# Storing u from ScalarE's queue, and moving late projections and splits, in a selective-scan and attention kernel

## The chip, the core and the metric

The kernel runs on one core of a Trainium2 chip. The metric is the device time of one execution in microseconds. Engines are named as in the profile: PE (TensorE), DVE (VectorE), ACT (ScalarE), POOL (GpSimd) and SP (SyncE, which here does nothing but issue DMAs).

## What is computed

An image batch x of shape (8, 64, 64, 96) goes through a state-space layer and then through an attention and feed-forward layer. The change lies in the first two of three passes, which compute this part of the reference:

```python
xz = jnp.einsum('bhwc,ec->bhwe', x, in_proj_w)          # x after a group norm
xin, z = jnp.split(xz, 2, axis=-1)
xc = jnp.transpose(xin, (0, 3, 1, 2))
xc = conv_general_dilated(xc, conv_w, ...) + conv_b      # depthwise, 3 x 3
xc = jax.nn.silu(xc)                                     # this is u
x_hw = xc.reshape(b, D_INNER, L)                         # row-major, o = 0
x_wh = jnp.transpose(xc, (0, 1, 3, 2)).reshape(b, D_INNER, L)   # column-major, o = 1
...                                                      # both, and both flipped: xs, K = 4
x_dbl = jnp.einsum('bkdl,kcd->bkcl', xs, x_proj_weight)  # dts, Bs, Cs
...
delta = jax.nn.softplus(dts + dt_projs_bias[None, :, :, None])
# the scan over L = 4096 steps, for 192 channels and 16 states
h = h * jnp.exp(d_t[..., None] * A) + (d_t * u_t)[..., None] * b_t[:, :, None, :]
y = jnp.einsum('bkdn,bkn->bkd', h, c_t)
```

The third pass (normalisation, gate, output projection, linear attention, quantised feed-forward layer) is the same in both kernels.

## The kernel before

**Three passes.** Pass 1 computes u, z and the projections x_dbl and puts them into DRAM. Pass 2 reads them back and does the scan. Pass 3 does the rest.

**Chunks.** Batches are taken in four pairs. The 192 channels of two batches make three chunks of 128 partitions (`chunk_rows`): chunks 0 and 1 hold the first 128 channels of one batch each ("one-batch chunks"), chunk 2 the last 64 channels of both ("two-batch chunk").

**Pass 1.** `projection` loads x, normalises it, multiplies by the input weights and copies the result into padded images (`xpad`, ScalarE) and z. `convolution` does nine multiply-adds on VectorE per chunk, in the order 0, 2, 1 within a pair, into one of four u buffers; then silu in two halves on ScalarE, then copies of u with rows and columns exchanged, in windows of 16 columns (`ut`, ScalarE; at the last chunk VectorE does them). `storage` stores the `ut` windows and then u itself in four column pieces, all through SyncE's queue. `x_projection` multiplies u by the projection weights on TensorE, ScalarE copies the product (`xd`), and SyncE stores it (`xd_d`). `split` loads rows of `xd_d`, makes three bf16 parts of them on ScalarE and GpSimd (`bq`, `bs`) and stores them (`b_d`, `dt_d`) for pass 2. A convolution takes a u buffer of four chunks earlier, and so waits until that chunk is stored and its x_proj is done. xpad, in turn, is free for the next pair when the convolution that read it is over.

**Pass 2.** It goes through 4 pairs x 3 chunks x 4 directions x 4 pieces of 1024 steps = 192 pieces, each with 16 states. For each piece: loads of the bf16 B rows (`xb`), of u, of `xdt`, and of C rows broadcast over the partitions (`c`); delta and the decay `da` (ScalarE); delta times u times B (`x`, `xg`, or on VectorE `wide`); the scan `h` (VectorE); h times C (`c<-c,h`, GpSimd); and the sum over the states on TensorE (`acc`). A two-batch chunk has the same work per piece, but loads each thing for two halves of the partitions and so issues twice the DMAs.

**Late work.** Some of pass 1's work is done within pass 2. The x_proj of batch 7 is there (`late_x_projection`, 16 units of 512 steps: three loads of u, four matmuls, a copy, a store), and so are the splits of batches 4 to 7 (`late_split`, 24 units). They belong to a kind "split" of which one unit is open at a time.

**What sets the order.** Each engine's instructions have a fixed order, written by a planner at build time (`weave`). The program parts are Python generators that name an engine, a cost and a delay before each step. Of all steps that could begin, `weave` takes the one that begins first by these costs; of those that begin at the same time, the one with the lower rank. In pass 1 the rank is the place of the unit's kind in the dictionary `room` (which also says how many units of a kind may be open), then its place in the list. In pass 2 the rank is a number: step n of piece `at` has about `at * N + n`, with N = 16, so a pair spans 768, a chunk 256. All of it concerns order alone; on the chip semaphores decide when an instruction begins. All engine instructions are issued by one helper, so the profile gives them one line, L93, and they are told apart by the names of their tiles.

Of the kernel before, what the change touches and what calls it, by code (L numbers as in the profile page):

```python
# [43 lines left out]
NB, HH, WW, C = 8, 64, 64, 96  # L44
L = HH * WW
DI, N, R, K = 192, 16, 6, 4
# [4 lines left out]
T = 1024  # L51
# [18 lines left out]
def chunk_rows(pair, c):  # L70

    b0 = 2 * pair
    if c < 2:
        return [(slice(0, P), b0 + c, slice(0, P))]
    return [(slice(64 * j, 64 * j + 64), b0 + j, slice(P, DI)) for j in range(2)]
# [225 lines left out]
def pass1(ctx, tc, g, a_neg, constants, ident, mhalf, engines, w_xp, u_d, z_d, xd_d, b_d, dt_d):  # L301
    nc = tc.nc
    pe, dve, act, pool = engines
    sp = InOrder(tc, nc.sync)
# [66 lines left out]
    sts, gms, us, turned, done = {}, {}, {}, {}, {}  # L371
# [115 lines left out]
    def convolution(pair, c):  # L487

        ty = c // 2
        src = xpad[c + pair % 2 if c == 2 else c]  # L490
        if pair == 0:
            yield ("parameters",)
        halves = 2 if pair == 0 and c == 0 else 1
        if halves == 1:
            for b in [2 * pair, 2 * pair + 1] if c == 2 else [2 * pair + c]:
                yield "proj", b
        before = {0: (pair - 1, 1), 2: (pair, 0), 1: (pair, 2)}[c]
        at = 3 * pair + ORDER.index(c) - UB
        if at >= 0:
            old, c_old = at // 3, ORDER[at % 3]  # L500
            for b in {0: (2 * old,), 1: (2 * old + 1,), 2: (2 * old, 2 * old + 1)}[c_old]:
                yield "xproj", b
            yield "stored", old, c_old
        if before[0] >= 0:
            yield "conv", *before
        u = None
        for part in range(halves):
            if halves > 1:
                for q in range(NG):
                    if q * RPG < (part + 1) * HH // halves + 1:  # L510
                        yield "projected", 0, q
            rows = slice(part * HH // halves, (part + 1) * HH // halves)
            for tap in range(9):
                end = yield "dve", (2.55 if tap == 0 else 4.55) / halves, 0.0
                if u is None:
                    u = us_p.tile([P, L], F32, name="u", tag=f"u{(at + UB) % UB}")
                    us[pair, c] = u
                    uv = u.rearrange("p (h w) -> p h w", w=WW)
                win = src[:, tap // 3 + rows.start : tap // 3 + rows.stop, tap % 3 : tap % 3 + WW]
                if tap == 0:  # L520
                    dve.tensor_scalar(uv[:, rows], win, conv_w[:, ty, tap : tap + 1], None, ALU.mult)
                else:
                    dve.scalar_tensor_tensor(uv[:, rows], win, conv_w[:, ty, tap : tap + 1], uv[:, rows], ALU.mult, ALU.add)
        done["conv", pair, c] = end
        for h in range(2):
            cols = slice(h * (L // 2), (h + 1) * (L // 2))
            end = yield "act", 2.0
            act.activation(u[:, cols], u[:, cols], AF.Silu, bias=conv_b[:, ty, :])
        done["u", pair, c] = end
        for i, (w, by_vector) in enumerate(windows(pair, c)):  # L530
            wide = w.stop - w.start
            tag = f"xn{i - 2}"
            step = ("dve", wide * 0.07, 0.3) if by_vector else ("act", 2.0, 0.3)
            if i < 2 or not by_vector:
                end = yield (*step, uts)
                tag = f"ut{uts.taken}"
            else:
                end = yield step
            turned[pair, c, i] = ut_p.tile([P, wide * HH], F32, name="ut", tag=tag), uts.taken
            (dve.tensor_copy if by_vector else act.copy)(turned[pair, c, i][0].rearrange("p (w h) -> p h w", h=HH), uv[:, :, w])  # L540
            done["turned", pair, c, i] = end

    def windows(pair, c):

        if (pair, c) == (NB // 2 - 1, ORDER[-1]):
            ends = (0, 16, 32, 40, 48, 56, 64)
        else:
            ends = (0, 16, 32, 48, 64)
        return [(slice(*at), len(ends) > 5) for at in zip(ends, ends[1:])]

    def storage(pair, c):

        parts, slow = chunk_rows(pair, c), 1 + c // 2 * 0.7
        for i, (w, by_vector) in enumerate(windows(pair, c)):
            yield "turned", pair, c, i
            end = yield "sp", 1.9 * (w.stop - w.start) / 16 * slow
            ut, of_ut = turned[pair, c, i]
            for part, b, ch in parts:
                sp.dma_start(u_d[b][1][ch, w.start * HH : w.stop * HH], ut[part, :])
            if i < 2 or not by_vector:  # L560
                uts.release(of_ut, end + 2.5)
        for i in range(4):
            cols = slice(i * T, (i + 1) * T)
            end = yield "sp", 1.9 * slow
            for part, b, ch in parts:
                sp.dma_start(u_d[b][0][ch, cols], us[pair, c][part, cols])
        done["stored", pair, c] = end + 2.5

    def x_projection(b, o, q):
        pair, j = b // 2, b % 2  # L570
# [32 lines left out]
    units = []  # L603
    for pair in range(NB // 2):
        batches = (2 * pair, 2 * pair + 1)
        for b in batches:
            units += [("stats", statistics(b, q)) for q in range(NG)]
            units.append(("norm", group_norm(b)))
            units += [("proj", projection(b, q)) for q in range(NG)]
        for c in ORDER:  # L610
            units.append(("conv", convolution(pair, c)))
            units.append(("store", storage(pair, c)))
        for b in batches:
            for o in range(2 if b < LATE_X else 0):
                units += [("xproj", x_projection(b, o, q)) for q in range(NG)]
                if b < LATE:
                    units += [("split", after(("xd", b, o), split((act, pool, sp), (two, two), 4.4, 4.0, xd_d[b][o], *w))) for w in splits(b, o, b_d, dt_d)]
    units += [("early", early_loads()), ("later", later_loads())]
    parts_of = [partial(us_p.tile, tag=f"u{UB - 1 - i}") for i in range(2)]
    units.append(("constants", make_constants(sp, dve, *parts_of, done)))  # L620
    room = {"early": 1, "proj": 4, "norm": 1, "stats": 5, "xproj": 4, "split": 2, "conv": 3, "store": 3, "later": 1, "constants": 1}
    weave([(kind, (list(room).index(kind), i), unit) for i, (kind, unit) in enumerate(units)], room, done)


# [1 line left out]
def pass2(ctx, tc, g, ident, engines, fixed, w_xp, u_d, xd_d, b_d, dt_d, y_d):  # L626
# [3 lines left out]
    pe, dve, act, pool = engines  # L630
    sp = InOrder(tc, nc.sync)
    room = {"da": 4, "h": 3, "x": 4, "xg": 1, "c": 6, "wide": 3, "acc": 1}
# [126 lines left out]
    def late_x_projection(b, o, q):  # L759

        yield "scans", 0
        pair, j = b // 2, b % 2
        cols = slice(q * GRP, (q + 1) * GRP)
        yield "sp", 1.8, 12.0
        ux = wide_late.tile([P, 2, GRP], F32, name="ux", tag="wide")
        sp.dma_start(ux[:, 0, :], u_d[b][o][0:P, cols])
        for i in range(2):
            sp.dma_start(ux[64 * i : 64 * i + 64, 1, :], u_d[2 * pair + i][o][P:DI, cols])
        yield "pe", 1.5, 0.2, slots["wide"]
        px, slot = take("wide", [P, T])  # L770
        for i, ty in enumerate((0, 1 + j)):
            pe.matmul(px[:, 0:GRP], w_xp[:, ty, o, :], ux[:, i, :], start=i == 0, stop=i == 1)
        end = yield "act", 0.58, 0.2
        xd = late_p.tile([P, GRP], F32, name="xd", tag="narrow")[0 : 2 * NXD]
        act.copy(xd, px[0 : 2 * NXD, 0:GRP])
        slots["wide"].release(slot, end)
        end = yield "sp", 0.7, 25.0
        sp.dma_start(xd_d[b][o][:, cols], xd)
        one_more(("xd", b, o), NG, end)

    def late_split(b, o, which):

        yield "scans", 0
        if b >= LATE_X:
            yield "xd", b, o
        yield from split((act, pool, sp), (late_p, wide_late), 1.25, 12.0, xd_d[b][o], *which)
        one_more(("split", b), 6, 0.0)
# [198 lines left out]
    units = []  # L986
# [23 lines left out]
                add("sum", -6, sum_over_n(at, n // 2), n)  # L1010
        add("acc", -2, take_acc(at), N)
    late_x = [(b, o, q) for b in range(LATE_X, NB) for o in range(2) for q in range(NG)]
    late = [("split", 3 * N * (i + 1), late_x_projection(*which)) for i, which in enumerate(late_x)]
    last = [(b, o, w) for b in range(LATE, NB) for o in range(2) for w in splits(b, o, b_d, dt_d)]
    late += [("split", 5 * N * (i + 1), late_split(*which)) for i, which in enumerate(last)]
    units += sorted(late, key=lambda unit: unit[1])
    weave(units, {"soft": 1, "prep": 1, "c": 1, "da": 2, "x": 1, "xg": 1, "dbu": 3, "scan": 3, "carry": 1, "term": 1, "sum": 1, "acc": 1, "split": 1}, done, keep_busy)

# [328 lines left out]
```

## Time and profile before

| | us |
|---|---|
| median of 3 runs (range) | 9731.19 (9728.52 to 9740.45) |
| the profiled execution, its own time | 9741.73 |
| its span in the profile | 9740.0 |
| DVE busy in the span | 9287.6 (95%) |
| ACT busy | 9098.2 (93%) |
| POOL busy | 8982.4 (92%) |
| PE busy | 7931.2 (81%) |
| first scan of pass 2 begins | 669.5 |
| last scan ends | 9056.3 |

Busy times are of the engines proper; issuing a DMA is not counted. Slices of the page divide the span into 40 equal parts, and a digit is the busy share in tenths. In lists of waits a row names the engine and the tile that an instruction writes, then what released it, and gives the total, the number of times and the longest. In timelines, the first two numbers are the start and the length in microseconds, and the bracket gives the idle time before the instruction and what ended it. `u_d<-u` are row-major stores of u, `u_d<-ut` those of the exchanged copies, `xd_d<-xd` those of x_proj.

### The profile page before, as it was taken

Reading aid. Unit: us, or ns where it says so; the run is one execution under the profiler, and the core shown is the slowest. Engines: PE = TensorE matmul, PEld = TensorE weight load, DVE = VectorE, ACT = ScalarE, POOL = GpSimd, SP = SyncE. Lnnn points to the kernel's source line nnn. Section 1 sums busy time; section 2 is a strip of 40 time slices with the busy share of each in tenths; the row PEclk is TensorE's granted clock in tenths of the full one; section 3 lists DMA queues with packets and bytes.
Section 4 is the critical chain, followed back from the end, with each engine's and each line's share of the span. In section 5 each row is a group of like instructions: output and inputs, shape, how many; then the busy total and the mean of one; then the engine's idle time right before and its main releaser. Section 6 shows DMA issues by size and latency. Waiting matters only on the chain.

```text
span 9740.0 us, 163473 instructions
## 1 busy us (share of the span) xinstructions
PE 7931.2 (81%) x57252; PEld 6142.7 (63%) x57252; DVE 9287.6 (95%) x6986; ACT 9098.2 (93%) x21482; POOL 8982.4 (92%) x2903
## 2 busy tenths in 40 slices
PE   7768888888888888888888888888888888888787
PEld 4336666666666666666666666666666666666676
DVE  8879999999999999999999999999999999999688
ACT  6669999999999999999999999999999999999787
POOL 1449999999999999999999999999999999999677
PEclk9879999999999999999999999999999999999898
DMA  6677776799987777799976767899867767999763
GB/s 179 211 233 226 235 236 225 239 224 209 217 224 224 230 231 226 237 211 214 214 232 221 237 217 226 228 211 210 224 222 233 227 220 230 219 208 214 195 183 111
DMA packets 945110, 2120.78 MB, mean 218 GB/s; under 512 B 278476, under 2 KB 426733, under 8 KB 944291
## 3 DMA queue, kind: packets, MB, share of 16 engines
q1 hardware_dynamic: 939394, 2108.50, 78.2%
q8 instruction: 458, 7.50, 0.3%
q14 instruction: 362, 2.96, 0.1%
q10 hardware_dynamic: 4464, 0.88, 0.1%
q0 software_dynamic: 432, 0.94, 0.0%
HBM read 1934.36 MB, written 175.66 MB: 217 GB/s over the span
## 4 chain that ended last, share of the span: by engine, by line
ACT 32%; DVE 24%; issue 17%; POOL 10%; PE 10%; DMA 6%; SPq 1%; DVEq 0%; POOLq 0%; ACTq 0%
DVE h L93 19%; ACT x L93 13%; ACT da L93 11%; POOL c L93 8%; PE wide L93 3%; DVE wide L93 3%; PE acc L93 3%; DMA c<-xd_d 2%; DMA xb<-b_d 1%; PE pa L93 1%; DMA xd_d<-xd 1%; ACT y L93 1%; ACT L93 1%; ACT delta L93 1%; ACT duT L93 1%
## 5 line engine op out<-in xcount | busy, mean ns | idle before, releaser
L93 POOL TENSOR_TENSOR c<-c,h 128x2048 f32<-128x2048 f32 x1536 | 6962.5, 4562 | 69.7 <-DVE h L93 48.7
L93 DVE TENSOR_TENSOR_SCAN h<-da,carry,wide 128x1024 f32<-128x1024 f32 x2304 | 5243.0, 2328 | 82.5 <-PE wide L93 39.6
L93 ACT ACTIVATE x<-duT,bT 128x128 f32<-128x128 f32 (+1 forms) x14336 | 4231.4, 368 | 2.1
L93 ACT ACTIVATE da<-delta,a_neg 128x1024 f32<-128x1024 f32 x3072 | 3508.2, 1146 | 171.2 <-DVE h L93 161.9
L93 PE MATMUL acc<-ident,c 128*128 128x128 f32 x24576 | 3132.4, 276 | 351.6 <-POOL c L93 342.6
L93 PEld LDWEIGHTS acc<-ident,c 128*128 128x128 f32 x24576 | 2762.0, 142 | 801.8 <-POOL c L93 687.5
L93 PE MATMUL wide<-ident,x 128*128 128x128 f32 x11264 | 1506.2, 277 | 418.9 <-DVE h L93 322.0
L93 DVE TENSOR_TENSOR_SCAN h<-da,wide 128x1024 f32<-128x1024 f32 x768 | 1704.9, 2268 | 43.6 <-PE wide L93 28.5
L93 PEld LDWEIGHTS wide<-ident,x 128*128 128x128 f32 x11264 | 1251.8, 142 | 690.6 <-DVE h L93 176.3
L93 DVE TENSOR_TENSOR wide<-du,wide 128x1024 f32<-128x1024 f32 x1216 | 1456.7, 1209 | 50.1 <-PE wide L93 47.5
L93 PE MATMUL acc<-sel,zero 96*128 96x512 bf16 x4100 | 1130.4, 380 | 0.0
L93 PE MATMUL wide<-xb,sel 96*128 96x512 bf16 x2432 | 722.8, 381 | 303.4 <-DVE h L93 263.8
L93 POOL TENSOR_TENSOR xg<-duT,bT 128x512 f32<-128x512 f32 (+1 forms) x640 | 895.9, 1417 | 20.5 <-ACT duT L93 20.5
L93 PE MATMUL wide<-ident,xg 128*128 128x128 f32 x3584 | 483.3, 279 | 153.8 <-DVE h L93 139.1
L93 PEld LDWEIGHTS <-zero 96*128 96x128 bf16 x4100 | 398.4, 98 | 317.2 <-issue 3.3
L93 PEld LDWEIGHTS wide<-ident,xg 128*128 128x128 f32 x3584 | 401.9, 143 | 244.4 <-issue 192.0
L93 PEld LDWEIGHTS <-sel 96*128 96x128 bf16 x2432 | 221.0, 98 | 498.0 <-issue 297.8
L93 POOL TENSOR_TENSOR du<-delta,u 128x1024 f32<-128x1024 f32 x192 | 458.3, 2387 | 29.2 <-DMA u<-u_d 27.0
L93 DVE SCALAR_TENSOR_TENSOR u<-xpad,conv_w,u 128x4096 f32<-128x4096 f32 (+1 forms) x104 | 446.1, 4290 | 2.4
L93 ACT ACT_TABLE_LOAD x197 | 252.8, 1283 | 38.2 <-DMA u_d<-u 22.8
L93 PE MATMUL wide<-ident,du 128*128 128x128 f32 x1536 | 204.7, 276 | 81.6 <-DVE h L93 65.1
L93 PE MATMUL px<-u,w_xp 128*128 128x512 f32 x448 | 216.1, 625 | 41.8 <-ACT u L93 21.0
(148 smaller groups left out, 6045.4 us busy)
## 6 DMA issues: line engine op xcount, KB each, us to landing
c<-xd_d SPq DMA_DIRECT2D x1024, 1024.0 KB
c<-xd_d SPq DMA_DIRECT2D x1024, 512.0 KB
u<-u_d SPq DMA_DIRECT2D x127, 512.0 KB
xdt<-dt_d SPq DMA_DIRECT2D x1146, 36.0 KB
xb<-b_d SPq DMA_DIRECT2D x382, 96.0 KB
u<-u_d SPq DMA_DIRECT2D x128, 256.0 KB
zs<-z_d SPq DMA_DIRECT2D x128, 256.0 KB
y_d<-y SPq DMA_DIRECT2D x96, 256.0 KB
```

Source lines behind the costliest of these rows:

```text
L93: ins = getattr(self.engine, op)(*args, **kwargs).ins
```

## The change

There are three edits in pass 1 and one in pass 2.

1. `storage` no longer stores row-major u. `convolution` does it, right behind the silu and ahead of the exchanged copies, from ScalarE's queue, with one DMA for a one-batch chunk (2 MB) and two for a two-batch chunk (1 MB each). The planner is told 0.7 us per issue and a delay of 10 us until the buffer counts as stored.
2. The storage units of the first three pairs get a place in `room` ahead of x_proj, split and conv. Those of the last pair become a kind of their own, "close", behind conv.
3. The late x_proj of batch 7 is ranked at `N * (1.9 * i + 1)`, so from 16 to 472: within the one-batch chunks of pair 0. Before, ranks went from 48 to 768, over the whole pair.
4. The late splits of batches 4 and 5 are ranked from 768 to 1208, those of 6 and 7 from 1536 to 1976: within the one-batch chunks of pairs 1 and 2. Before, the 24 ranks went from 80 to 1920 in steps of 80.

```diff
@@ convolution
         done["u", pair, c] = end
+        parts = chunk_rows(pair, c)
+        end = yield "act", 0.7 * len(parts), 10.0
+        for part, b, ch in parts:
+            act.dma_start(u_d[b][0][ch], u[part])
+        done["stored", pair, c] = end
@@ storage
-        for i in range(4):
-            cols = slice(i * T, (i + 1) * T)
-            end = yield "sp", 1.9 * slow
-            for part, b, ch in parts:
-                sp.dma_start(u_d[b][0][ch, cols], us[pair, c][part, cols])
-        done["stored", pair, c] = end + 2.5
@@ pass1
-            units.append(("store", storage(pair, c)))
+            units.append(("store" if pair < NB // 2 - 1 else "close", storage(pair, c)))
...
-    room = {"early": 1, "proj": 4, "norm": 1, "stats": 5, "xproj": 4, "split": 2, "conv": 3, "store": 3, "later": 1, "constants": 1}
+    room = {"early": 1, "proj": 4, "norm": 1, "stats": 5, "store": 3, "xproj": 4, "split": 2, "conv": 3, "close": 3, "later": 1, "constants": 1}
@@ pass2
-    late = [("split", 3 * N * (i + 1), late_x_projection(*which)) for i, which in enumerate(late_x)]
+    late = [("split", N * (1.9 * i + 1), late_x_projection(*which)) for i, which in enumerate(late_x)]
     last = [(b, o, w) for b in range(LATE, NB) for o in range(2) for w in splits(b, o, b_d, dt_d)]
-    late += [("split", 5 * N * (i + 1), late_split(*which)) for i, which in enumerate(last)]
+    late += [("split", N * (48 * (i // 12 + 1) + 2.5 * (i % 12)), late_split(*which)) for i, which in enumerate(last)]
```

## The prediction

> **What bounds the kernel now.** I read the page's slices first, then the busy times of stretches cut at the pass borders, then who waits for whom inside pass 1, then the chunks of pass 2. The slices show three regimes:
>
> ```profile
> DVE  8879999999999999999999999999999999999688
> ACT  6669999999999999999999999999999999999787
> POOL 1449999999999999999999999999999999999677
> ```
>
> The stretches give them sizes (columns: length, busy us of PE, PEld, DVE, ACT, POOL, clock, DMA share, GB/s):
>
> ```profile
> 493.00:626.00 133.00, 83.99 (x187) 35.71 (x188) 120.00 (x28) 87.77 (x101) 34.85 (x16) 0.80 0.66 211
> 626.00:670.00 44.00, 13.24 (x52) 7.93 (x51) 7.05 (x12) 13.86 (x14) 4.29 (x4) 0.65 0.80 257
> 670.00:9056.00 8386.00, 6908.20 (x51688) 5447.00 (x51688) 8229.67 (x4286) 8129.90 (x19578) 8292.70 (x2414) 0.99 0.82 224
> ```
>
> Pass 2 is 8386 of 9740 us, and there VectorE, ScalarE and GpSimd are all near 98%: only a stage with idle time of all three can give anything. Pass 1 (to about 670) has no full engine: the chain runs through VectorE's convolutions (39 us a chunk) and whatever holds the next one up. From 626 to 670 nobody works and the DMA engines are at their densest: pass 1 ends in a drain of stores. The change touches nothing after 9056.
>
> What VectorE waits for in pass 1 (total us, times, longest):
>
> ```profile
> DVE u L93 <- ACT xpad L93: 20.8, 3, 9.6
> DVE u L93 <- DMA u_d<-u: 18.3, 2, 13.0
> ```
>
> What ScalarE waits for there:
>
> ```profile
> ACT xd L93 <- DMA xd_d<-xd: 54.6, 41, 6.4
> ...
> ACT ut L93 <- DMA u_d<-ut: 32.4, 18, 5.7
> ACT L93 <- DMA u_d<-u: 22.8, 1, 22.8
> ```
>
> So late stores stop VectorE directly, and stop ScalarE, whose xpad copies VectorE waits for. The last row is the end of the pass, in ScalarE's timeline:
>
> ```profile
> 635.49 3.89 ACT L93 ACTIVATE u<-u,conv_b 128x2048 f32<-128x2048 f32 x2
> ...
> 664.64 1.28 ACT L93 ACT_TABLE_LOAD   x1 [22.83 <-DMA u_d<-u]
> ```
>
> The last silu ends at 639.4, and the first decay of pass 2 waits until the last row-major u store has landed at 664.6.
>
> **Part 1, the u store on ScalarE's queue.** Removed from SyncE: 32 issues of 512 KB and 32 of 256 KB. Added on ScalarE: 8 issues of 2 MB and 8 of 1 MB, right behind the silu. The bytes are the same.
>
> Where the stores stand on the path. (a) Today they come far behind their silu: chunk 2 of pair 1 had its silu at 281 and was stored between 372 and 447. The convolution that takes its buffer (pair 2, chunk 1) stands 13.0 us for it, and starts at 451.5. Stored behind the silu that wait is gone; next late is the x_proj of batch 3, which reads the same buffer until about 435, and VectorE is busy with statistics to 438.5. So I take all 13 us. The other store waits of a convolution (5.3 us at 498.6, 3.6 at 333.0) are worth nothing: the convolution after each starts late anyway, because xpad is late (6.5 and 9.6 us).
> (b) Between the end of each pair's last convolution and the middle chunk of the next pair lie 177.3-232.9, 329.4-384.5 and 493.4-548.7, each 55 us, with ScalarE busy 42 to 48 of 56. ScalarE is the chain there; its waits for landings in them add to 3.8, 8.5 and 5.3, together 17 us (x_proj stores, split loads, transposed stores, all on SyncE's queue). With 64 issues fewer on that queue, and the transposed stores ranked ahead of x_proj, I take two thirds: 12 us.
> (c) The end. From 635.9 SyncE issues 6.5 MB of stores, landed at 664.6: 28.7 us, about 237 GB/s. Of these, 2 MB are row-major u of chunk 2, whose silu was over at 600; they now leave before the last convolution ends, under which the DMA share is 0.66. 4.5 MB remain, 20 us at the same rate, so the landing comes near 658: 7 us. The last silu itself stands 10 us behind its convolution, behind x_proj copies that wait for their stores 1.5 us each; those stores stay, so I give that 2 us. Together 9 us.
>
> What it costs ScalarE. The only issues of this kind in the trace are SyncE's:
>
> ```profile
> L93 SPq DMA_DIRECT2D u_d<-u x64: 341/706/2702, 123.5 to 658.3; - x64
> ```
>
> An issue takes 0.3 to 2.7 us. A 2 MB issue isn't in the trace; 1 MB loads of c issue in 0.4 us when nothing is in the way, so size is not what sets it, congestion is. And there is a new wait: in the trace's DMA records SyncE's and ScalarE's issues take eight completion semaphores in turn, and each stands until the last transfer on its semaphore has landed. Stores of 512 KB landed in 3.5 to 8.8 us, median 5.2, by those semaphores. So an issue on ScalarE may cost from 0.3 us (the eighth transfer before it has landed) to 11.5 us (8.8 + 2.7). Behind it are queued the transposed copies, xpad, xn and z of the next batch, and the x_proj copies, and TensorE and VectorE wait for those. I take 2.7 us, an issue at its dearest but rarely a landing, because ScalarE comes to its store some 4 us after the convolution's end. One such store lies in each of the stretches of (b): 3 x 2.7 = 8 us; those outside are covered by ScalarE's 30 to 40% idle time under convolutions. In turn SyncE's eighth issue behind a 2 MB store waits for it; SyncE waited 197 us for ScalarE in pass 1, which covers that.
>
> A rule speaks against all this. The Trainium skill (DMA: Bandwidth & Descriptors, section "Issuing engines are not separate DMA queues") says that transfers started by different engines run on the same 16 DMA engines and interleave, so another issuer saves only issue time. By it (a) to (c) hold only as far as the *order* of stores changes, and SyncE's saved issue time (64 x 0.7 = 45 us) is on no path: taken strictly 0 us. The rows decide for the order: the 13.0 us wait is for a store 91 us or more behind its silu, at a DMA share of 0.69. Where the share is 0.80, at the end, I follow the rule and count bytes only.
>
> Pass 1: 13 + 12 + 9 - 8 = 26 us less. Ends: 13 + 17 + 21 with no cost, some 50 less; and below nothing, see the rivals.
>
> **Part 2, late work in one-batch chunks.** Pass 2 by chunk, cut at the first scan of each:
>
> ```profile
> 1358.80:2042.90 684.10, 569.61 (x4307) 449.25 (x4305) 679.41 (x354) 660.47 (x1474) 682.66 (x184) 1.00 0.75 234
> 2042.90:2789.80 746.90, 604.25 (x4359) 467.00 (x4359) 699.49 (x370) 720.37 (x1969) 717.34 (x246) 0.97 0.98 214
> ...
> 5574.50:6255.30 680.80, 562.61 (x4299) 446.99 (x4297) 678.72 (x353) 655.59 (x1463) 675.51 (x177) 1.00 0.73 226
> 6255.30:6975.30 720.00, 589.62 (x4317) 456.26 (x4316) 699.49 (x370) 710.82 (x1948) 710.77 (x240) 0.99 0.98 214
> ```
>
> The first and third are one-batch chunks (pairs 0 and 2), the second and fourth two-batch ones. Pair 0's two-batch chunk takes 746.9 us, pair 2's 720.0, with VectorE equally busy (699.5): 26.9 us of plain idle time. Only the first carries late work (5 late x_proj, 3 splits). Two-batch chunks run at a DMA share of 0.98: the late 5 x 0.5 MB of u, 0.9 MB of xd and 1.8 MB of splits are 5.2 MB, 24 to 25 us at 214 GB/s (1 MB a little over 10^6 bytes). SyncE's waits there agree:
>
> ```profile
> SPq L93 <- DMA xd_d<-xd: 24.4, 4, 9.4
> ...
> SPq L93 <- ACT xd L93: 11.1, 3, 4.3
> SPq L93 <- DMA b_d<-bs: 7.6, 1, 7.6
> ```
>
> Behind these SyncE holds the xb and u of the next piece, for which all three engines stand 5 to 6 us at 2254, 2290 and 2569. The change puts none of this there: 26 us saved.
>
> What it costs elsewhere. Pair 0's one-batch chunks lose 6 splits and take 16 x_proj instead of 11, each 4 matmuls and one copy of 0.6 us, with ScalarE idle 24 us and the DMA share 0.75: nothing by the row at 1358.8, which with 5 x_proj and 3 splits is only 3.3 us over the empty chunk at 5574.5. So without splits they win 3.3 us each, 6.6. A split is 2 x 1.17 us on GpSimd, which has 5 us to spare in an empty chunk. Pair 1's one-batch chunks with 6 splits each take 691.0 and 689.0 against 682.8 and 680.7 in pair 3: 8.3 us for 6, 1.4 a split. Twelve splits now fall on pair 1's (7 and 5 by rank, as before about 12) and twelve on pair 2's (before 2): about 10 more at 1.4, 13 to 14 us. Sum: 26 + 6.6 - 13.5 = 19 us less. Ends: 8 (x_proj every 30 ranks instead of 48 disturbs its chunks) and 27 (splits fall into ScalarE's and GpSimd's gaps).
>
> **The sum.** The profiled run is 9741.7 us with a span of 9740.0; it is 10.5 over the median of 9731.2. 26 + 19 = 45: a span near 9695, and 9731 - 45 = 9686 as a median. A measurement of this kernel tells about 0.2%, 19 us, from no change.
>
> **Rivals.**
> - *Order buys nothing in pass 1* (the rule strictly, or ScalarE pays as much as it wins): only part 2, 9712, within 0.2%. For it: the same bytes, a DMA share near 0.7. Against: the 13.0 us wait at 451. Chance 0.17.
> - *The queue was the pass's real limit*: ScalarE's 105 us of waits for x_proj stores, transposed stores and split loads mostly go, 55 us in pass 1 with part 2 at 24: 9652. Chance 0.2.
> - *Late work is moved, not removed*: one-batch chunks pay the 26 us back; pass 1 alone, 9705. Against: the 3.3 us of the chunk at 1358.8. Chance 0.12.
> - *Slower*: ScalarE stands at its store for a semaphore whose transfer SyncE issued late. Price up to 11.5 us; half of the 16 issues on the path are 92 us, against 34 + 19 won: 9770. It decides from 53 / 8 = 6.6 us a store. For it: SyncE's issues take up to 3.9 us in bursts. Against: a median landing of 5.2 us. Chance 0.08.
> - My forecast has 0.43, with 9665 to 9705 as its own range.
>
> Faster by over 0.2%: 0.43 + 0.2 + 0.12 = 0.75; within 0.17; slower 0.08. The range 9645 to 9722 takes in the first three rivals at their values and leaves out the slower one and the far end of the second.
>
> **What would show it.** The convolution now at 451.5 starts behind x_proj, not behind a u store; ScalarE's waits for landings fall from 105 us; the gap now 22.8 before the first decay is about 15; the first scan, now at 669.5, comes near 644; pair 0's two-batch chunk takes about 720 us, pair 2's one-batch chunks 687 to 692. I am wrong if ScalarE shows long gaps before its u stores, or if the three 55 us stretches grow.

## The result and the profile after

The changed kernel takes 9709.1 us (median of 12 runs, 9699.6 to 9720.1) against 9732.4 for the kernel before (12 runs beside it). The ratio is 0.9975, 95% interval 0.9966 to 0.9984: 23 us less, between 16 and 33. The forecast was 45 less.

Both profiled executions lie some 10 us above their medians (9720.1 and 9741.7), so they can be set beside each other. The slices of the page after hardly differ from before:

```profile
DVE  8879999999999999999999999999999999999687
ACT  5669999999999999999999999999999999999787
POOL 1459999999999999999999999999999999999777
```

Cut at the last convolution, the first scan and the last scan (columns as before):

```profile
493.00:633.00 140.00, 91.00 (x210) 39.46 (x208) 120.23 (x26) 85.04 (x110) 64.51 (x18) 0.82 0.65 194
633.00:673.50 40.50, 7.29 (x40) 5.51 (x40) 8.63 (x12) 17.35 (x19) 11.41 (x14) 0.58 0.82 245
673.50:9038.60 8365.10, 6901.12 (x51737) 5444.10 (x51738) 8231.73 (x4288) 8127.22 (x19575) 8289.72 (x2414) 0.99 0.82 224
```

Pass 2 is 21.7 us shorter (8386.8 to 8365.1), with the same busy times. In these two executions pass 1 is not shorter at all: its last convolution ends at 632.9 instead of 625.7 and the first scan begins at 673.5 instead of 669.5. In the first stretch GpSimd is busy 64.5 us instead of 34.9. One execution is a weak witness for a few microseconds: the work behind the last scan, which is the same in both kernels, differs by 3.9 us here (683.7 and 679.8), and a second execution of the same pass 1, in run a2 below, began its first scan at 664.0.

The four chunks of pass 2 that answer to those shown before (pair 0, then pair 2, each the second one-batch chunk and the two-batch chunk):

```profile
1361.50:2046.20 684.70, 573.93 (x4331) 455.25 (x4330) 679.74 (x354) 658.53 (x1470) 676.40 (x179) 1.00 0.74 233
2046.20:2764.90 718.70, 586.35 (x4337) 451.46 (x4338) 699.18 (x370) 712.65 (x1951) 714.00 (x243) 1.00 1.00 215
5547.80:6237.90 690.10, 570.28 (x4322) 455.07 (x4320) 679.86 (x353) 661.51 (x1480) 687.89 (x188) 0.99 0.72 228
6237.90:6959.20 721.30, 596.50 (x4324) 466.59 (x4322) 699.26 (x370) 714.01 (x1954) 712.16 (x241) 0.97 0.98 214
```

The second row is the gain: 746.9 to 718.7. The third is the price, 680.8 to 690.1, in a chunk that now does splits on GpSimd (675.5 to 687.9 busy). Both repeat: the eleven other runs with the new late ranks have 716.7 to 721.5 and 689.5 to 690.4 there, and a2, with the old ones, 741.2 and 681.1. SyncE's waits in the second row's chunk no longer hold a row for `xd`, `xd_d` or `bs`. In pass 1, VectorE's waits from 60 to 670:

```profile
DVE u L93 <- ACT xpad L93: 38.2, 3, 18.8
DVE ut L93 <- DMA u_d<-ut: 27.0, 2, 13.7
```

The row `DVE u <- DMA u_d<-u` (18.3 us before) is gone, and that for xpad has grown by 17.4 (20.8 to 38.2): almost the same time is now waited for something else. ScalarE's waits up to 670:

```profile
ACT xd L93 <- DMA xd_d<-xd: 57.9, 31, 10.4
ACT bs L93 <- DMA bq<-xd_d: 32.4, 9, 8.4
...
ACT ut L93 <- DMA u_d<-ut: 15.9, 11, 3.6
...
ACT delta L93 <- PE wide L93: 14.8, 1, 14.8
```

Fewer stores on SyncE's queue did not shorten the waits for x_proj's stores (54.6 to 57.9). Those for exchanged stores halved (32.4 to 15.9), and those for split loads nearly doubled (17.8 to 32.4). The new issues are cheap; among the rows that touch `u_d`, with durations in ns as least/median/most:

```profile
L93 ACTq DMA_DIRECT2D u_d<-u x16: 321/416/1310, 93.6 to 645.4; - x16
```

**Where the lead goes.** In the kernel before, the convolution at 498.6 ended at 542.2; now it runs from 486.8 to 526.9. So at that point VectorE is 15.3 us ahead: step (a) arrived there in full. Its timeline after that point, before:

```profile
548.72 2.36 DVE L93 TENSOR_SCALAR u<-xpad,conv_w 128x4096 f32<-128x4096 f32 x1 [6.54 <-ACT xpad L93]
551.11 36.13 DVE L93 SCALAR_TENSOR_TENSOR u<-xpad,conv_w,u 128x4096 f32<-128x4096 f32 x8
...
```

and after:

```profile
545.75 2.35 DVE L93 TENSOR_SCALAR u<-xpad,conv_w 128x4096 f32<-128x4096 f32 x1 [18.85 <-ACT xpad L93]
548.14 40.77 DVE L93 SCALAR_TENSOR_TENSOR u<-xpad,conv_w,u 128x4096 f32<-128x4096 f32 x8
...
592.11 40.79 DVE L93 SCALAR_TENSOR_TENSOR u<-xpad,conv_w,u 128x4096 f32<-128x4096 f32 x8
```

x8 are the eight multiply-adds of one convolution. The lead falls from 15.3 to 3.0 us in one wait for xpad (18.85 us instead of 6.54), and to 7.2 us behind in two convolutions whose multiply-adds take 5.10 us in the mean (40.77 / 8) instead of 4.52. Taken one by one, twelve of the sixteen last 5.26 us and four 4.49; before, all sixteen lasted 4.49. Beside these two convolutions GpSimd now does splits, the last of which begins at 643.5; before, the last began at 546.3.

Why xpad comes hardly earlier than before stands in the chain of waits of the kernel after (start, length, what):

```profile
370.39 11.28 DMA xt<-in_x
...
520.47 9.66 DMA xt<-in_x
```

These are loads of x, issued by SyncE; 2 MB stores of u had left ScalarE's queue at 367.0 and 516.9. TensorE's projection waits for them, and xpad for the projection. Over pass 1, by the completion semaphores of the trace, the 7 loads `xt<-in_x` issued from 1 us before to 5 us after a u store land in 9.8 us on average, the other 37 in 3.9; the stores of z in 10.4 (12 of them) and 4.1. Before, with u stores of 256 and 512 KB, both groups of loads took 3.7 to 3.8. So the load at 520.5 explains some 6 of the 12.3 us by which the lead shrank in the wait for xpad; the rest of them is not traced.

The chain as a whole, in shares of the stretch from 330 to the first scan, before:

```profile
by line: DMA xd_d<-xd 25.1%; PE pa L93 17.6%; PE px L93 11.5%; DMA u_d<-ut 8.0%; ACT ut L93 4.8%; ACT u L93 4.6%; SPq L93 4.1%; issue 4.1%; PE pt L93 3.6%; DMA bq<-xd_d 2.3%; DMA c<-xd_d 2.2%; DMA u<-u_d 2.2%; ACT xd L93 2.1%; ACT z L93 1.6
```

and after:

```profile
by line: SPq L93 15.5%; PE pa L93 12.2%; DMA xd_d<-xd 11.2%; DMA u_d<-ut 9.7%; PE px L93 9.6%; issue 6.9%; DMA xt<-in_x 6.1%; DMA bq<-xd_d 5.3%; POOL bs L93 4.1%; ACT ut L93 3.7%; ACT xd L93 1.9%; PE pt L93 1.7%; DMA dt_d<-bs 1.6%; POOL bq 
```

(The view cuts such lines off.) The landings of x_proj's stores take less of the chain: 25.1% of 340 us is 85, 11.2% of 344 is 39. SyncE's own issuing comes in (14 to 53 us), loads of x (21), split loads (8 to 18) and splits on GpSimd (14). And no convolution, `DVE u`, is a piece of either chain in this stretch: in the kernel before, the wait of 13.0 us at 451 was not a part of the chain that ended the pass.

**The end of pass 1.** ScalarE's timeline:

```profile
645.35 0.33 ACTq L93 DMA_DIRECT2D u_d<-u  x1
645.71 1.28 ACT L93 ACT_TABLE_LOAD   x1 [0.39 <-ACT u L93]
661.81 1.11 ACT L93 ACTIVATE delta<-wide,dt_b 128x1024 f32<-128x1024 f32 x1 [14.82 <-PE wide L93]
```

and VectorE's:

```profile
646.23 1.05 DVE L93 COPY ut<-u 128x1024 f32<-128x1024 f32 x1 [13.33 <-DMA u_d<-ut]
660.93 4.93 DVE L93 COPY ut<-u 128x1024 f32<-128x1024 f32 x5 [13.65 <-DMA u_d<-ut]
```

The old wait for `u_d<-u` (22.83 us) is gone. In its place the last exchanged copies stand 13.65 us for an earlier transposed store, and ScalarE stands 14.82 us. From the end of silu to the first scan it was 30 us, and is 28.

### The profile page after: what moved, and what is told of

Read it like the earlier page. It is cut to its first block, busy times and chain, and to the rows that moved or that the text cites. A ratio compares the mean times of both kernels' runs of the same rounds, so it can differ in the third digit from the quotient of the medians.

```text
span 9718.4 us, 163491 instructions
## 1 busy us (share of the span) xinstructions
PE 7933.6 (82%) x57300; PEld 6145.1 (63%) x57300; DVE 9300.3 (96%) x6986; ACT 9095.1 (94%) x21482; POOL 8987.4 (92%) x2903
## 4 chain that ended last, share of the span: by engine, by line
ACT 31%; DVE 24%; issue 17%; POOL 10%; PE 9%; DMA 5%; SPq 1%; DVEq 0%; POOLq 0%; ACTq 0%
DVE h L93 19%; ACT x L93 13%; ACT da L93 11%; POOL c L93 8%; PE wide L93 4%; DVE wide L93 3%; PE acc L93 3%; DMA c<-xd_d 1%; ACT y L93 1%; ACT L93 1%; SPq L93 1%; ACT delta L93 1%; DMA xb<-b_d 1%; ACT duT L93 1%; POOL xg L93 1%
## 5 line engine op out<-in xcount | busy, mean ns | idle before, releaser
L93 POOL TENSOR_TENSOR du<-delta,u 128x1024 f32<-128x1024 f32 x192 | 459.6, 2394 | 23.5 <-ACT delta L93 13.1
L93 POOL TENSOR_TENSOR bq<-bq,bs 128x512 f32<-128x512 f32 (+1 forms) x48 | 104.9, 2188 | 205.2 <-ACT bs L93 205.2
L93 PE MATMUL px<-u,w_xp 128*128 128x512 f32 x448 | 226.5, 645 | 57.8 <-ACT u L93 34.6
```

Source lines behind the costliest of these rows:

```text
L93: ins = getattr(self.engine, op)(*args, **kwargs).ins
```

## The experiments

The kernel before, run beside them, took 9733.9 (runs a), 9735.8 (b1 and runs c) and 9732.6 (runs d and b3).

| run | median us | from before | ratio (95%) |
|---|---|---|---|
| a1_late_only | 9715.2 | -18.7 | 0.9980 (0.9971 to 0.9989) |
| a2_pass1_only | 9721.7 | -12.3 | 0.9986 (0.9980 to 0.9993) |
| a3_by_sp | 9681.3 | -52.6 | 0.9948 (0.9935 to 0.9960) |
| a4_old_ranks | 9702.6 | -31.3 | 0.9968 (0.9956 to 0.9979) |
| b1_pieces | 9750.0 | +14.2 | 1.0015 (1.0008 to 1.0021) |
| c1_sp_order_act_issue | 9704.8 | -31.0 | 0.9972 (0.9961 to 0.9983) |
| c2_act_order_sp_issue | 9696.4 | -39.4 | 0.9964 (0.9952 to 0.9977) |
| c3_by_sp_old_ranks | 9701.6 | -34.2 | 0.9967 (0.9956 to 0.9978) |
| d1_last_pair_sp | 9700.7 | -31.9 | 0.9971 (0.9959 to 0.9982) |
| d2_first_pairs_sp | 9697.1 | -35.5 | 0.9968 (0.9956 to 0.9981) |
| b3_conv_first | 9712.3 | -20.4 | 0.9981 (0.9974 to 0.9987) |
| d3_sp_split_first | 9697.3 | -35.3 | 0.9967 (0.9955 to 0.9978) |

An interval is 6 to 12 us to each side, and a profiled execution can lie 14 us from its median (c1); so medians judge the runs, and profiles only what repeats in several.

### The two halves: a1_late_only and a2_pass1_only

a1 is the kernel before with the two changed lines of `pass2` alone; a2 is the changed kernel with the old ones back:

```diff
-    late = [("split", 3 * N * (i + 1), late_x_projection(*which)) ...]
+    late = [("split", N * (1.9 * i + 1), late_x_projection(*which)) ...]
-    late += [("split", 5 * N * (i + 1), late_split(*which)) ...]
+    late += [("split", N * (48 * (i // 12 + 1) + 2.5 * (i % 12)), late_split(*which)) ...]
```

> Pass 1 as before, only the ranks of the late work of pass 2 are changed. Theory (all of the gain is the late work): the first scan stays at 669 to 671 us, the two-batch chunk of pair 0 falls from 747 to 717 to 722 us, and the whole is 19 to 24 us shorter than before. Rival (pass 1 gave part of the gain and the profiled run of the changed kernel hides it): only 8 to 14 us shorter.

> Only the edits of pass 1; late work ranked as before. Theory: the wait of the convolution at 451 is gone (about 20 us), but transfers behind a u store land some 6 us later and the splits of pass 1 end near 643, so the first scan comes at 670 to 676 us and the whole is within 6 us of before. Rival (the edits do what was forecast, and only the profiled run was unlucky): first scan at 640 to 655, 15 to 30 us shorter.

a1: 18.7 us less, first scan at 669.6, pair 0's two-batch chunk 721.1 us, pair 2's second chunk 689.7. a2: 12.3 us less (7 to 19), with pair 0's two-batch chunk at 741.2. The expectation for a2, no more than 6 us from before, missed: the edits of pass 1 do gain a little. The sum of 31 agrees with 23 (16 to 33). So most of the gain is the late work, and pass 1 gives 12 by a2, or 23.3 - 18.7 = 5 by the difference, where 26 were forecast.

a2 has the changed kernel's pass 1, instruction for instruction, and so shows how far two executions of it differ. Its last convolution ends at 628.9 and its first scan begins at 664.0, 4.0 and 9.5 us earlier than in the profile of the change. Its chain from 330 to the first scan does hold one convolution (43.7 us):

```profile
by line: PE pa L93 13.7%; DVE u L93 13.1%; DMA xd_d<-xd 12.9%; PE px L93 11.5%; SPq L93 10.3%; DMA u_d<-ut 9.2%; DMA xt<-in_x 6.2%; issue 4.6%; DMA bq<-xd_d 2.5%; ACT ut L93 2.4%; PE pt L93 1.9%; ACT xd L93 1.8%; POOL bs L93 1.6%; DVE ut L9
```

So several chains of pass 1 are so nearly equal that small differences between executions decide which ends last, and two first scans less than some 10 us apart tell nothing.

### Issuer and ranks: a3_by_sp and a4_old_ranks

a3 is the changed kernel with the u store a step of SyncE, still behind the silu; a4 is it with the old `room` and one kind of storage:

```diff
# a3
-        end = yield "act", 0.7 * len(parts), 10.0
+        end = yield "sp", 0.7 * len(parts), 10.0
-            act.dma_start(u_d[b][0][ch], u[part])
+            sp.dma_start(u_d[b][0][ch], u[part])
# a4
-    room = {..., "stats": 5, "store": 3, "xproj": 4, "split": 2, "conv": 3, "close": 3, ...}
+    room = {..., "stats": 5, "xproj": 4, "split": 2, "conv": 3, "store": 3, ...}
```

> As the changed kernel, but the u store behind the silu is issued by SyncE, in one DMA a part, with the same cost for the planner. Theory (what costs is 2 MB in one burst, whoever issues it): SyncE's next transfers are behind it in the same queue and land 5 to 8 us later too; first scan 668 to 680 us. Rival (ScalarE's queue is the harm[...]): SyncE's transfers near a store land as the others do, about 4 us for a load of x, and the first scan comes 8 us or more earlier than 673.

> As the changed kernel, but storage has its old place in the ranks of pass 1, behind x_proj, split and conv, for all pairs. Theory A (the ranks push the splits of pass 1 to its end, where GpSimd works beside the last two convolutions and the first loads of pass 2 come late): the last split ends near 550 instead of 645, the last two convolutions take 38 us instead of 43, first scan at 650 to 664. Theory B (the burst of the store alone): first scan within 5 us of 673.

a3 is the best kernel of the study: 52.6 us less than before, its interval (39 to 63) apart from the change's (16 to 33). Its first scan is at 646.7. The same early store, in the same large DMAs, earns some 29 us more when SyncE has it, in order and in queue, than when ScalarE has; the theory that the burst costs the same whoever issues it is out. a4 may gain 8 us on the change, inside the intervals; in it the last split of pass 1 begins at 578, and the last convolution is back at 38.2 us, but the first scan, at 665.4, comes no earlier than that of a2.

### Large DMA or second queue: b1_pieces

The changed kernel, with ScalarE storing u in four column pieces, each a step of its own:

```diff
-        end = yield "act", 0.7 * len(parts), 10.0
-        for part, b, ch in parts:
-            act.dma_start(u_d[b][0][ch], u[part])
+        for i in range(4):
+            cols = slice(i * T, (i + 1) * T)
+            end = yield "act", 0.7 * len(parts), 10.0
+            for part, b, ch in parts:
+                act.dma_start(u_d[b][0][ch, cols], u[part, cols])
```

> As the changed kernel, but ScalarE stores u in four column pieces (512 KB, or 2 x 256 KB), each a planner step of its own, so that other ScalarE work can lie between them. Theory of the burst: SyncE's loads of x near a store land in 4 to 6 us instead of 9.8, first scan 5 to 20 us earlier, whole 9690 to 9704. Rival (the burst costs nothing on the path, the order does): within 6 us of 9709, or slower by ScalarE's 48 further issues of 0.5 us.

The burst is indeed gone: x loads near a store land in 4.9 us, the others in 4.0. But the kernel is 37.5 us slower than the change by the differences to before, with the first scan at 705.6. VectorE's waits, 60 to 705:

```profile
DVE st L93 <- PE pt L93: 45.3, 15, 24.3
DVE ut L93 <- DMA u_d<-u: 36.4, 1, 36.4
```

The last piece leaves ScalarE at 686.3, 41 us later than the last store of the change. Forty-eight steps in ScalarE's order (64 issues), each placed by the planner, spread the store out, and VectorE's last exchanged copies wait 36.4 us behind it. So this run says nothing for or against small pieces as such, and the burst alone is not what makes a version slow.

### Order and queue apart: c1, c2 and c3

c1 plans the u store as SyncE's step and issues it from ScalarE; c2 plans it as ScalarE's and issues it from SyncE; c3 is a3 with the old `room` of a4:

```diff
# c1
-        end = yield "act", 0.7 * len(parts), 10.0
+        end = yield "sp", 0.7 * len(parts), 10.0
# c2
-            act.dma_start(u_d[b][0][ch], u[part])
+            sp.dma_start(u_d[b][0][ch], u[part])
```

> The u store is planned as a step of SyncE, as in the kernel that stores by SyncE and took 9681, so that the order of all other instructions is the same; but ScalarE issues it. Theory (the order decides, not the issuing engine): within 8 us of 9681, first scan 640 to 655. Rival (the second queue is the harm, since its 2 MB come beside loads that SyncE issued earlier): 9697 or more, within 8 us of the changed kernel's 9709.

> The reverse: planned as a step of ScalarE, so that the order is the changed kernel's, but issued by SyncE. Theory (order decides): within 8 us of 9709. Rival (queue decides): 9693 or less; loads of x behind a store land in about 4 us instead of 10.

> Stored by SyncE behind the silu, planned so, and storage with its old rank (the two single edits that were each faster than the changed kernel). If the gains are of different causes (28 and 7 us): 9670 to 9678. If both only reorder the same steps: anything from 9675 to 9705, without a sum.

| us from before | issued by SyncE | issued by ScalarE |
|---|---|---|
| planned as SyncE's | -52.6 (a3) | -31.0 (c1) |
| planned as ScalarE's | -39.4 (c2) | -23.3 (the change) |

The traces confirm that within a row of this table all other instructions of pass 1 have the same order. At equal order ScalarE's queue costs 21.6 and 16.1 us, and at equal queue ScalarE's order costs 13.2 and 7.7. Each difference alone is uncertain by some 15 us to each side. The two for the queue are each just beyond that and agree, so the queue's cost is clear; the two for the order are within it, and so is their mean (10 us, with 11 to each side), so the order's cost is likely, not shown. Neither expectation, order alone or queue alone, fits both runs. A companion of the order: within -1 to +5 us of a u store, a3 and c1 issue none and one of their loads of x, c2 and the change ten and seven.

c3 shows that gains do not add: a3 is 29 and a4 8 us under the change, both together 11. With SyncE's queue the old ranks harm (18 us); with ScalarE's they may help (8 us, inside the intervals). Why is not shown.

### Where the queue costs: d1_last_pair_sp and d2_first_pairs_sp

```diff
# d1
-            act.dma_start(u_d[b][0][ch], u[part])
+            (sp if pair == NB // 2 - 1 else act).dma_start(u_d[b][0][ch], u[part])
# d2
+            (sp if pair < NB // 2 - 1 else act).dma_start(u_d[b][0][ch], u[part])
```

> The changed kernel with the u stores of the last pair only (chunks 0, 2, 1 of pair 3) issued by SyncE; the planned order is the same. With all twelve by SyncE it was 16 us faster than the changed kernel (-39 against -23 us from before). Theory 'tail': the queue matters where pass 1 drains; then this run keeps most of it, -35 to -40 us from before, and the gap from the last silu to the first scan falls from 28 to about 23 us. Rival 'middle': ScalarE's queue harms by the stores that land beside loads and x_proj stores of the first three pairs; then this run stays within 5 us of the changed kernel, -20 to -28.

> The opposite half: u stores of the first three pairs issued by SyncE, those of the last pair from ScalarE's queue. Theory 'tail': -20 to -28 us from before, as the changed kernel. Rival 'middle': -35 to -40, and the last convolution begins some 10 us earlier than the 588.8 of the changed kernel. If both halves gain about 8, the cost is spread.

Against the change, d1 gains 8.6 and d2 12.2 us, c2 (both) 16.1. That looks like a cost spread over both halves, but each gain is uncertain by some 15 us. The end of pass 1 can be read directly. VectorE's last exchanged copies in d2, where ScalarE issues the last u store:

```profile
642.76 4.92 DVE L93 COPY ut<-u 128x1024 f32<-128x1024 f32 x5 [12.69 <-DMA u_d<-ut]
```

in d1, where SyncE does:

```profile
641.28 2.82 DVE L93 COPY ut<-u 128x1024 f32<-128x1024 f32 x5 [4.89 <-DMA u_d<-ut]
```

and in c2, as in d1:

```profile
639.24 2.81 DVE L93 COPY ut<-u 128x1024 f32<-128x1024 f32 x5 [3.20 <-DMA u_d<-ut]
```

With ScalarE's queue this wait is 13.65 (the change), 14.12 (a2), 12.69 (d2) and 11.82 (c1); with SyncE's 4.89 (d1), 3.20 (c2) and 3.31 (a3). From the end of silu to the first scan it takes 28.2, 29.9, 28.6 and 28.1 us in the first four, 22.8, 23.0 and 20.2 in the others. On SyncE's queue the two transposed stores that the copies wait for are issued just ahead of the u store and land in 4.4 to 5.6 us; where ScalarE issues the u store, it leaves within 1.3 us of them, and they land in 13.1 to 15.3. That is 6 us of the queue's cost, shown four times against three. With the old ranks there is little of it: in a4 the transposed stores leave 2 to 6 us ahead of ScalarE's u store and land in 7.8 to 8.5 us, the wait is 1.30, and from silu to first scan it takes 22.6 us (20.4 in c3, with SyncE's queue). So the harm lies in leaving together from two queues.

For the first three pairs the trace has only a companion: x loads near a u store land in 9.8 and 10.1 us where ScalarE issues it (the change, d1), in 7.5 and 7.3 where SyncE does (c2, d2); for stores of z it is 10.4 and 10.6 against 9.5 and 9.1. Whether this makes up d2's 12 us is not shown.

### The place of convolution and splits: b3_conv_first and d3_sp_split_first

```diff
# b3: the changed kernel
+    room = {..., "stats": 5, "conv": 3, "store": 3, "xproj": 4, "split": 2, "close": 3, ...}
# d3: a3_by_sp
+    room = {..., "stats": 5, "split": 2, "store": 3, "xproj": 4, "conv": 3, "close": 3, ...}
```

> The changed kernel with the convolution's steps (silu, u store and exchanged copies with it) ranked ahead of storage, x_proj and split in pass 1. Theory 'ranks': in the changed kernel the new rank of storage lets silu and u store slip behind x_proj copies, and the convolutions before each pair's end are late for that; ahead of them, silu and store follow at once, and the run gains 10 us or more on the changed kernel: -33 or better. Rival 'queue': the harm is the store beside SyncE's transfers, whatever its place; then -15 to -28.

> The u store issued by SyncE as its own planned step behind the silu (-53 us from before with the changed ranks), and besides the splits of pass 1 ranked ahead of storage. Theory 'splits at the end': in the changed kernel splits run on GpSimd to 643, slow the last two convolutions from 38 to 43 us each and delay the loads for the first scan; earlier splits give 5 to 15 us more, -58 to -68, and the last convolutions are near 39. Rival 'order is a lottery of the plan': the splits take TensorE's and ScalarE's places elsewhere in the pass, and it gives -30 to -53.

b3 shows that the last convolution alone does not set the end of pass 1. Its last convolution ends at 601.7, 31 us before the change's, and its last silu at 610.9, 34 us earlier; its first scan is at 669.0. GpSimd's timeline shows what ends the pass instead:

```profile
598.59 4.09 POOL L93 TENSOR_TENSOR bs<-bq,bs 128x512 bf16<-128x512 f32 x1 [5.73 <-ACT bs L93]
...
622.69 1.15 POOL L93 TENSOR_TENSOR bs<-bq,bs 128x512 bf16<-128x512 f32 x1 [0.73 <-ACT bs L93]
...
645.04 1.15 POOL L93 TENSOR_TENSOR bs<-bq,bs 96x512 bf16<-96x512 f32 x1 [0.73 <-ACT bs L93]
646.13 3.25 POOL L93 DMA_DIRECT2D xdt<-dt_d  x6
```

The splits, which wait for loads of x_proj's results, now run last, and the loads for pass 2 are queued behind them. (b3 reorders the splits too, so it isn't a test of an early convolution with all else equal.) The theory that late silus ate the gain is refuted: -20.4 us, where it wanted -33 or better.

d3 is the counterpart. Splits first do bring the last two convolutions back to 38.2 us each, so GpSimd beside them was the cause of the 43 to 44. But d3 is 17 us worse than a3, whose last convolution takes 43.8, and so misses the 5 to 15 us that were expected. Shorter convolutions at the end did not help a3. Where d3 loses, its trace does not settle: in the profiled execution its first scan, at 642.8, is even before a3's, and pass 2 takes 7 us longer in the same work.

## Why the prediction was half right

**The sign was right, the sum twice too large:** 23 us less instead of 45. The median of 9709 lies outside the forecast's own 9665 to 9705; it lies in the wider 9645 to 9722 because that range takes in the rivals. The rival "order buys nothing in pass 1" gave 9712, within 3 us of what happened. That is luck in part: a2's pass 1 does gain 12 us (7 to 19), and a3 shows that order and queue can buy much more.

**Part 2 was right in mechanism and in its sum.** Forecast 19 us; a1 gave 18.7, and pass 2 in the profile 21.7. The main term came: pair 0's two-batch chunk was to be near 720, and is 718.7. (It had carried six late x_proj before, not five: six copies `xd` begin in it.) "Late work is moved, not removed" is thereby out. Two small terms missed and nearly cancel. The 6.6 us for pair 0's one-batch chunks did not come: 689.2 to 688.0, and 684.1 to 684.7. And of pair 2's one-batch chunks, both forecast at 687 to 692, only the second rose, 680.8 to 690.1; the first, with eight split operations on GpSimd instead of three, went from 684.9 to 683.2. Price 7.7 us instead of 13.5.

**Part 1 failed in its premise, "the chain runs through VectorE's convolutions".** From it came step (a), "I take all 13 us". The wait did vanish, as forecast, and VectorE was 15.3 us ahead at 526.9. But the chain from 330 to the first scan holds no convolution in the profile before, nor in that of the change. b3 moves the end of the last convolution by 31 us, and the first scan by 4.5 between two profiles, less than two executions of one pass 1 differ. Pass 1 has several chains of nearly the same length (convolution, projection with x loads, x_proj with its stores, splits): in a2, the same pass 1, `DVE u` is 13.1% of the chain, and in c2, with the change's order, 13.4%.

**Step (b), 12 us from ScalarE's landing waits in the three 55 us stretches,** was wrong in its ground. The waits for landings are 58 + 32 + 16 = 106 us instead of falling from 105. Two of the three stretches grew, as the prediction named for being wrong: 51.2, 57.8 and 58.8 us. It counted issues taken off SyncE, and not what a burst of 2 MB does to transfers that start beside it (loads of x in 9.8 us instead of 3.9).

**Step (c), 9 us at the end,** had the old wait right, but a new one took its place, 13.65 us for a transposed store. Silu to first scan went from 30 to 28 us.

**The cost on ScalarE was over-sized.** The 2.7 us taken for a store were 0.42 in the median and 1.31 at most, 16 issues together some 8 us. So the rival "slower", with ScalarE standing at its store, was wrong in its mechanism. SyncE does stand for semaphores of u stores now (23.1 us in six waits in pass 1), as the prediction allowed.

**The rule that was weighed** (the Trainium skill, DMA: Bandwidth & Descriptors, "Issuing engines are not separate DMA queues") gave, taken strictly, 0 us for another issuer. For pass 1 as a whole that was nearer than the 26. But the section names only a saving, and at equal order ScalarE's queue *costs* 16 to 22 us. The early store with its new ranks is worth 34 us on SyncE's queue (a3 is that much under a1), and on ScalarE's 5 to 12.

**Missed:** the last splits of pass 1 move from 546 to 643, beside the last convolutions. Two thirds of that is the new rank of storage: a4, with the old one, has the last split at 578. The prediction named the ranks only as help for (b).

**What stays open** is how the rest of the queue's cost, 10 to 15 us, is made up in the first three pairs; why the changed ranks help SyncE's version by some 18 us and not ScalarE's; and which of pass 1's nearly equal chains a faster version would have to shorten.

## What to carry to other kernels

A wait that a change removes is worth time only if its instruction is in the chain of the stretch that sets the end; read that chain before adding waits up, and where several chains are nearly equal, forecast little. Moving large stores to a second queue can take away the order in which they landed: here small stores that had gone ahead then landed beside them, in 13 to 15 us instead of 4 to 6. Try the earlier store on the old queue first: here, planned and issued there, it was worth 29 us more.

## What the runs showed of the hardware

- A small transfer issued from 1 us before to 5 us after a 1 or 2 MB store lands some 6 us later: x loads 9.8 instead of 3.9 us, z stores 10.4 instead of 4.1, exchanged stores 14.1 (3 of them) instead of 5.1 (all in the changed kernel). With the big store on the same queue (c2, d2) it is less for x loads, 7.3 to 7.5, and hardly less for z stores, 9.1 to 9.5.
- Issuing a DMA of 1 to 2 MB costs ScalarE no more than one of 256 to 512 KB cost SyncE: median 0.42 us here, 0.71 there.
- VectorE and GpSimd slow each other, and not in proportion: a multiply-add of the convolution takes 4.49 us alone, and beside splits either 4.49 or 5.26 (the last two convolutions of the changed kernel; the one at 498.6 in the kernel before has the same two values). d3, whose splits come first, has 4.49 throughout in its last two. A split's operation on GpSimd takes 4.09 us beside a convolution (at 598.6 in b3) and 1.15 after it.
